# Six x buffers, loads five slots ahead, and a re-ordered beginning in a recurrent block with a looked-up feed-forward part

## The chip, the core and the metric

The kernel runs on one core of one Trainium2 chip. The metric is the device time of one execution in microseconds (us). Before the change the median of three runs is 2197.28 us (2196.02 to 2201.48).

A core has a matrix engine (PE, with its weight loads shown as PEld), VectorE (DVE), ScalarE (ACT), GpSimd (POOL), and SyncE (SP), which here only issues transfers. Each engine works through its own instructions in order. A transfer is issued by one of them (nearly all of them by SP) and is then carried out by the core's 16 DMA engines.

## What is computed

For x of 8 batches with 1024 rows of 512 numbers, cut to what matters:

```python
xn = layernorm(x)
q = xn @ Wq;  gate = softmax(xn @ Wg)
for i in range(3):
    k, v = xn @ Wk[i], xn @ Wv[i]
    w = decay[i] ** max(diff - 1, 0) * (diff > 0)     # diff = s - t, so only later rows count
    blended += gate[..., i:i+1] * (((q @ k.T) * w) @ v)
s = blended @ Wo * out_scale
g = silu(ffn(xn))       # ffn: silu(xn @ lut[gate_idx].T) * (xn @ lut[up_idx].T), then @ lut[down_idx].T
out = x + s * g
```

`lut` has 16 entries. The three feed-forward matrices (1376 x 512, twice, and 512 x 1376) exist only as integer indices into it.

## The kernel before

`phase_1` (L505) computes the attention part of all eight batches and, beside it, builds the feed-forward matrices. `phase_2` (L580) computes the feed-forward part and the result.

**Phase 1 is a hand-written interleaving of Python generators.** A batch has eight tiles of 128 rows (c = 7 down to 0). The loop at L544 runs over batches b = 0 to 8, and inside it the loop at L547 runs over eight slots k. In each slot several generators take a step:

- `newer` is `project(b)` (L278). In slot k it transposes tile c = 7-k (L325, matmuls `pt`, copied to `xnT` by ACT), normalizes tile c-1 (L317), takes the mean and variance of tile c-2 (`statistics`, L299), and loads tile c-3 (`load`, L295). The tiles of x have four buffers (`xp`, L513), so a load can start once the tile four places earlier has been transposed. In a later part of the slot come `features` (L361, matmuls `pq`, from slot 4 on) and `values` (L331, matmuls `pv`). For b = 0, `values` runs one slot late (`lag`). Batch 0 takes statistics and normalizes on DVE, the others on ACT; both use POOL for the reciprocal root (`rstd`).
- `softmax` (L340) turns four tiles' gate logits into weights on DVE and ACT. It then writes them, transposed, to DRAM (`gTd<-g`, L355: 1536 words of 4 bytes) and reads them back broadcast over partitions (`ga<-gTd`, L359).
- `older` is `chunks(b-1)` (L428): the recurrence of the batch before, matmuls `pk`, `psc`, `pu`, `po`. `gated` (L437) multiplies `ga` by q on DVE. The first `psc` of a batch waits for it.
- `ending` is the last part of `project(b-1)` (L415): `features(0, k)`, the sums `ts` for phase 2, and the transfers `xsd<-xnT` and `xsd<-ts` (L424 to L426).
- `following` is `project(b+1)`; it takes its first two steps in slots 6 and 7, and its first step ends in the statistics of its tile 7.
- `setup` is `tables` (L128): the powers of the decay, written to DRAM (`powd<-k_tab`, L152) and read back (`back<-powd`, L158) for `w_tab` and `q_tab`.
- `weights` (L524) builds the matrices: `gate_up_weights` (L205), then `down_weights` (L249). Each tile loads its indices (`idx`, two buffers), looks them up on DVE in 19 steps (`look_up`, L171), makes sums on POOL, and writes to DRAM (`wgud`, `quadd`, `wdd`). `build_some(n)` takes n steps of it.

**Order.** At the end, `keep_order` (L918) ties PE, DVE, ACT and POOL to the order in which Python emitted their instructions. SP is tied only up to L543, before the first slot; the transfers emitted later are put into SP's queue by the scheduler. SP issues its queue strictly in order: a transfer that waits for its data holds up everything behind it.

**Beginning.** L538 to L542 take the first steps: `newer` twice (tiles 7, 6, 5 and 4 are loaded), `more` twice (L91: first `wvg_sb` on ACT's queue, then `wqk_sb` and `wo_sb` on SP's), and `setup` once. From slot 0 on, `weights` takes a step per slot, so the look-up's first instruction (L176) stands on DVE in slot 0.

**Phase 2** begins with the load `xs<-xsd` (L599), whose memory is that of `xnT` and `ts` of phase 1. So it waits for the last `xsd<-ts`.

Of the kernel before, what the change touches and what calls it, by code (L numbers as in the profile page):

```python
# [18 lines left out]
P = 128  # L19
# [19 lines left out]
def recurrent_block(ctx: ExitStack, tc, x, wq, wk, wv, wo, wg, decay_logits, out_scale, lut, gidx, uidx, didx, out):  # L39
# [51 lines left out]
    def more_weights(wvg_sb, wqk_sb):  # L91
        nc.scalar.dma_start(out=wvg_sb[:, :, NI * D :], in_=wg.rearrange("(c p) d -> p c d", p=P))
        for i in range(NI):
            nc.scalar.dma_start(
                out=wvg_sb[:, :, i * D : (i + 1) * D], in_=wv[i].rearrange("(c p) d -> p c d", p=P)
            )
        yield
        nc.sync.dma_start(out=wqk_sb[:, :, :D], in_=wq.rearrange("(c p) d -> p c d", p=P))
        for i in range(NI):
            nc.sync.dma_start(  # L100
                out=wqk_sb[:, :, (i + 1) * D : (i + 2) * D], in_=wk[i].rearrange("(c p) d -> p c d", p=P)
            )
        nc.sync.dma_start(out=wo_sb, in_=wo)


# [22 lines left out]
    def tables():  # L128
# [21 lines left out]
        nc.gpsimd.tensor_tensor(c_tab, dec, e_c, ALU.pow)  # L150
        with nc.allow_non_contiguous_dma(reason="384 words, once"):
            nc.sync.dma_start(out=pow_d[:, P:].rearrange("i s -> s i"), in_=k_tab)  # L152
        for _ in range(3):
            yield
        backs = []
        for step, first in ((1, 0), (0, P)):
# [4 lines left out]
            backs.append(back)  # L161
        for _ in range(2):
            yield
        for tab, back in zip((w_tab, q_tab), backs):
# [39 lines left out]

    def gate_up_weights(build, pool, pair_pool):  # L205

        for o, (s, m) in enumerate(OCH):  # L210
            n = 2 * NV * m
            idx = build.tile([P, NB], I32, name="idx", tag="idx", bufs=2)
            iv = idx[:, :n].rearrange("p (a b) -> p a b", b=m)
            gs, us = (src[:, s : s + m].rearrange("(c p) b -> p c b", p=P) for src in (gidx, uidx))
            nc.sync.dma_start(out=iv[:, 2:6, :], in_=gs)
            nc.sync.dma_start(out=iv[:, 0:2, :], in_=us[:, 0:2, :])
            nc.sync.dma_start(out=iv[:, 6:8, :], in_=us[:, 2:4, :])
            wf = pool.tile([P, 2 * NB], F32, name="wgu", tag="wgu", bufs=2)
            yield from look_up(build, wf[:, :n], idx[:, :n], P, n)
            w = wf[:, : 2 * n].rearrange("p (k two m) -> p k two m", two=2, m=m)  # L220
            a21, a11, a12, a22, s1, s2, s3, s4 = (w[:, k] for k in range(8))
            nc.gpsimd.tensor_tensor(s1, a21, a22, ALU.add)
            nc.gpsimd.tensor_tensor(s2, s1, a11, ALU.subtract)
            yield
            nc.gpsimd.tensor_tensor(s3, a11, a21, ALU.subtract)
            nc.gpsimd.tensor_tensor(s4, a12, s2, ALU.subtract)
            nc.sync.dma_start(out=wgu_d[o], in_=wf[:, 2 * m : 2 * n].rearrange("p (a b) -> p a b", b=m))
            if o < 4 * NQ:
                if o % 2 == 0:
                    upper = w[:, 1:]  # L230
                    continue
                lower = w[:, 1:]
                to = quad_d[o // 4][:, :, o // 2 % 2, :].rearrange("p k (t m) -> p k t m", m=P)
                pair = pair_pool.tile([P, 7, 4, P], F32, name="pair", tag="pair")
                nc.sync.dma_start(out=to[:, :, 0:2, :], in_=upper)
                nc.sync.dma_start(out=to[:, :, 2, :], in_=lower[:, :, 1, :])
                b21, b22, b11, b12 = lower[:, :, 0], lower[:, :, 1], upper[:, :, 0], upper[:, :, 1]
                nc.gpsimd.tensor_tensor(pair[:, :, 0], b21, b22, ALU.add)
                yield
                nc.gpsimd.tensor_tensor(pair[:, :, 1], pair[:, :, 0], b11, ALU.subtract)  # L240
                yield
                nc.gpsimd.tensor_tensor(pair[:, :, 2], b11, b21, ALU.subtract)
                yield
                nc.gpsimd.tensor_tensor(pair[:, :, 3], b12, pair[:, :, 1], ALU.subtract)
                nc.sync.dma_start(out=to[:, :, 3:7, :], in_=pair)
                for _ in range(3):
                    yield

    def down_weights(build, pool):  # L249

        s, m = OCH[-1]
        idx = build.tile([P, NB], I32, name="idx", tag="idx", bufs=2)
        nc.sync.dma_start(out=idx[:m, :V], in_=didx[s : s + m, :])
        wf = pool.tile([P, 2 * NB], F32, name="wgu", tag="wgu", bufs=2)
        yield from look_up(build, wf[:m, :V], idx[:m, :V], m, V)
        nc.sync.dma_start(out=wdt_d, in_=wf[:m, :V])
        for j in range(NK):
            idx = build.tile([P, NB], I32, name="idx", tag="idx", bufs=2)
            for a in range(2):
                nc.sync.dma_start(out=idx[:, ts(a, V)], in_=didx[ts(j + a * NK, P), :])  # L260
            t = pool.tile([P, 2 * NB], F32, name="wgu", tag="wgu", bufs=2)
            yield from look_up(build, t[:, : 2 * V], idx, P, 2 * V)
# [5 lines left out]
            nc.gpsimd.tensor_tensor(t4, b21, t2, ALU.subtract)  # L268
            nc.sync.dma_start(out=wd_d[j], in_=t[:, : 7 * V // 2])

# [7 lines left out]
    def project(b, pools, sides, kept):  # L278
# [61 lines left out]
        def softmax(hf):  # L340
# [12 lines left out]
            nc.vector.tensor_tensor(g, g, sm.to_broadcast([P, n, NI]), ALU.mult)  # L353
            with nc.allow_non_contiguous_dma(reason="1536 words"):
                nc.sync.dma_start(  # L355
                    out=gT_d[b][ts(hf, n * NI), :].rearrange("k p -> p k"), in_=g.rearrange("p c i -> p (c i)")
                )
            gates.append(att.tile([P, n * NI, P], F32, name=f"ga{b}_{hf}", tag="ga"))
            nc.sync.dma_start(out=gates[-1], in_=gT_d[b][ts(hf, n * NI), :].partition_broadcast(P))  # L359

# [11 lines left out]

        load(NC - 1)
        if b > 0:
            load(NC - 2)
            statistics(NC - 1)
        yield
        if b == 0:
            load(NC - 2)
        load(NC - 3)  # L380
        if b == 0:
            load(NC - 4)
            statistics(NC - 1)
        normalize(NC - 1)
# [3 lines left out]
        for k in range(NC):  # L388
            c = NC - 1 - k
            transpose(c)  # L390
            if c > 0:
                normalize(c - 1)
            if c > 1:
                statistics(c - 2)
            if c > 2 and (b, k) != (0, 0):
                load(c - 3)
            if b == 0 and k == 0:
                warm_up(5)
            yield
            if k >= NC // 2:  # L400
                features(1, k - NC // 2)
            half = softmax(1) if k == NC // 2 + lag else iter(())
            next(half, None)
            yield
            next(half, None)
            if k >= lag:
                values(c + lag)
            if lag and k == NC - 1:
                values(0)
            yield  # L410
# [14 lines left out]
        nc.sync.dma_start(out=xs_d[b][:, 4:6, :], in_=b22)  # L425
        nc.sync.dma_start(out=xs_d[b][:, 6:14, :], in_=ts_.rearrange("p a b u -> p (a b) u"))  # L426

# [77 lines left out]
    def phase_1():  # L505
        nonlocal small, p_a, p_c, p_r
        with (
# [4 lines left out]
            tc.tile_pool(name="tp", bufs=1) as tp,  # L512
            tc.tile_pool(name="xp", bufs=4) as xp,  # L513
            tc.tile_pool(name="wts", bufs=1) as wts,
# [8 lines left out]
            pools = (xp, xnp, tp, att)  # L523
            weights = chain(gate_up_weights(build, wgup, pairp), down_weights(build, wgup))  # L524
            wvg_sb = wts.tile([P, NV, NI * D + NI], F32, name="wvg_sb", tag="wvg_sb")
# [15 lines left out]
            next(setup)  # L541
            next(more, None)  # L542
            keep_order(tc, seen, (mybir.EngineType.SP,))  # L543
            for b in range(B + 1):  # L544
                following = project(b + 1, pools, (wvg_sb, wqk_sb), kept) if b + 1 < B else iter(())
                older = chunks(b - 1, (chk, blp), kept) if b else iter(())
                for k in range(NC):  # L547
                    next(older, None)
                    next(newer, None)
                    next(setup, None)  # L550
                    busy = (b > 0 or k >= NC // 2) and b < B
                    build_some(1 + (0 < b < B))
                    if k < NC // 2:
# [8 lines left out]
                    if k >= NC - 2:  # L562
                        next(following, None)
                    next(newer, None)
                    next(older, None)
                for g in (older, ending):
                    for _ in g:
                        pass
                ending, newer = newer, following
            for _ in weights:  # L570
                pass


# [386 lines left out]
```

## Time and profile before

| what | value |
|---|---|
| median of three runs | 2197.28 us |
| the profiled execution: its own time | 2197.51 us |
| its span, first to last instruction | 2195.7 us |
| PE busy | 2171.0 us, 99% |
| DVE, ACT, POOL busy | 51%, 38%, 42% |
| first feed-forward matmul of phase 2 (`fs`) | 627.53 us |
| first matmul that multiplies data (`pt`) | 6.08 us |

All positions below are us from the span's start. The windows view gives the busy time of each engine in a stretch, with its number of instructions, and then the granted PE clock (1.00 is full speed), the busy share of the DMA engines and GB/s. The chain of waits goes back from the last instruction to what released each step. A timeline row is start, length, engine, line, operation, output<-input and shapes; a bracket gives the idle time before it and what ended it.

### The profile page before, as it was taken

How to read it: one execution, taken by the hardware profiler on the slowest of the kernel's cores; microseconds unless marked ns; L12 is line 12 of the kernel's file. 1: busy time of each engine (PE TensorE's matmuls, PEld its weight loads, DVE VectorE, ACT ScalarE, POOL GpSimd, SP SyncE). 2: the span in 40 equal slices, each digit the busy share in tenths (PEclk: the TensorE clock that was granted, in tenths of full speed). 3: DMA queues.
4: the chain of work that ended last, by engine and by line, in shares of the span. 5: the costliest groups of instructions: out<-in, count | busy, mean ns of one | idle time of the engine just before them, and what ended most of it. 6: DMA issues, size and time to landing. Idle time of an engine off the chain costs nothing.

```text
span 2195.7 us, 25271 instructions
## 1 busy us (share of the span) xinstructions
PE 2171.0 (99%) x9234; PEld 1599.3 (73%) x9234; DVE 1111.9 (51%) x1589; ACT 830.0 (38%) x1795; POOL 912.6 (42%) x800
## 2 busy tenths in 40 slices
PE   8989999999999999999999999999999999999998
PEld 5656666666668778678858876885787678578867
DVE  5866868688635534433533443353344335433533
ACT  3556666666434214312421441243144124313410
POOL 2525454334243454424525441543445153434512
PEclk9999999999999999999999999999999999999999
DMA  5766655534284424334432442343244234234501
GB/s 140 203 160 212 162 163 181 181 125 170 83 327 151 149 99 154 114 115 139 161 122 82 153 130 106 132 155 105 105 154 147 106 116 151 89 132 147 164 24 53
DMA packets 137153, 305.29 MB, mean 139 GB/s; under 512 B 50147, under 2 KB 71910, under 8 KB 136006
## 3 DMA queue, kind: packets, MB, share of 16 engines
q1 hardware_dynamic: 127190, 279.03, 39.1%
q0 software_dynamic: 7728, 23.86, 3.0%
q8 instruction: 73, 1.20, 0.2%
q10 hardware_dynamic: 2112, 0.79, 0.1%
q14 instruction: 50, 0.41, 0.1%
HBM read 225.72 MB, written 77.93 MB: 138 GB/s over the span
## 4 chain that ended last, share of the span: by engine, by line
PE 94%; DMA 3%; DVE 1%; POOL 1%; issue 1%; ACT 1%; ACTq 0%; SPq 0%; POOLq 0%; DVEq 0%
PE s L677 27%; PE ds L821 22%; PE fs L631 9%; PE pq L368 8%; PE pv L335 6%; PE sE L677 4%; PE fsE L631 4%; PE po L488 3%; PE ds L832 2%; PE ps L843 2%; PE psc L466 2%; PE pu L474 1%; PE pt L328 1%; DMA x<-in_x 1%; PE pk L457 1%; DMA xs<-xsd 1%
## 5 line engine op out<-in xcount | busy, mean ns | idle before, releaser
L677 PE MATMUL s<-xs,wq 128*128 128x256 f32 x2688 | 602.9, 380 | 0.0
L677 PEld LDWEIGHTS s<-xs,wq 128*128 128x128 f32 x2688 | 508.7, 190 | 78.4 <-DVE sE L704 2.7
L821 PE MATMUL ds<-wd,s 128*128 128x256 f32 x1280 | 286.7, 379 | 0.0
L821 PEld LDWEIGHTS ds<-wd,s 128*128 128x128 f32 x1280 | 243.2, 190 | 33.0
L368 PE MATMUL pq<-xnT,wqk_sb 128*128 128x512 f32 x512 | 230.3, 592 | 0.0
L821 PE MATMUL ds<-wd,h 128*128 128x256 f32 x960 | 222.9, 379 | 0.0
L821 PEld LDWEIGHTS ds<-wd,h 128*128 128x128 f32 x960 | 182.3, 190 | 52.5 <-issue 27.0
L631 PE MATMUL fs<-xs,wr 128*128 128x512 f32 (+1 forms) x480 | 215.4, 592 | 0.3 <-DMA xs<-xsd 0.3
L733 POOL TENSOR_TENSOR u<-u,e 128x512 f32<-128x512 f32 x64 | 79.9, 1270 | 276.0 <-DVE u L729 276.0
L335 PE MATMUL pv<-wvg_sb,xnT 128*128 128x387 f32 x512 | 179.6, 493 | 7.4 <-ACT xnT L329 7.4
L700 DVE TENSOR_TENSOR s<-s,e 128x512 f32<-128x512 f32 x112 | 78.4, 700 | 187.6 <-ACT s L699 187.6
L631 PEld LDWEIGHTS fs<-xs,wr 128*128 128x128 f32 (+1 forms) x480 | 86.8, 181 | 116.1 <-issue 112.4
L368 PEld LDWEIGHTS pq<-xnT,wqk_sb 128*128 128x128 f32 x512 | 92.3, 190 | 91.8 <-issue 91.8
L846 POOL TENSOR_TENSOR gx<-gx 128x512 f32<-128x512 f32 x63 | 80.3, 1275 | 184.6 <-DVE gx L844 141.1
L335 PEld LDWEIGHTS pv<-wvg_sb,xnT 128*128 128x128 f32 x512 | 93.8, 193 | 63.2 <-ACT xnT L329 7.6
L314 POOL TENSOR_SCALAR rstd<-rstd 128x1 f32<-128x1 f32 x56 | 26.9, 481 | 258.8 <-ACT junk L313 258.2
L615 POOL TENSOR_TENSOR xs<-xs 128x1792 f32<-128x1792 f32 (+1 forms) x38 | 127.9, 3382 | 7.6 <-issue 6.6
L704 DVE TENSOR_TENSOR sE<-s,e 128x512 f32<-128x512 f32 x112 | 78.3, 699 | 85.9 <-PE s L677 85.9
L862 ACT ACTIVATE gx<-ds 128x256 f32<-128x256 f32 x32 | 12.3, 384 | 287.1 <-PE ds L832 287.1
L677 PE MATMUL sE<-xs,wq 128*128 128x256 f32 x448 | 115.0, 379 | 0.0
L695 ACT COPY e<-sE 128x512 f32<-128x512 f32 x112 | 65.6, 586 | 123.7 <-PE sE L677 123.7
L737 POOL TENSOR_TENSOR h<-h,e 128x512 f32<-128x512 f32 x64 | 80.0, 1273 | 57.4 <-issue 46.4
(146 smaller groups left out, 3248.6 us busy)
## 6 DMA issues: line engine op xcount, KB each, us to landing
wq<-quadd SPq DMA_DIRECT2D x112, 896.0 KB, 4.5
xs<-xsd SPq DMA_DIRECT2D x8, 3584.0 KB, 12.1
x<-in_x SPq DMA_DIRECT2D x64, 256.0 KB, 5.2
xsd<-ts SPq DMA_DIRECT2D x8, 2048.0 KB, 7.8
gx<-in_x SPq DMA_DIRECT2D x64, 256.0 KB, 2.9
out<-gx POOLq DMA_DIRECT2D x63, 256.0 KB, 2.3
wr<-wgud SPq DMA_DIRECT2D x16, 896.0 KB, 4.6
ga<-gTd SPq DMA_DIRECT2D x16, 768.0 KB, 5.1
```

The costliest lines, as they stand in the source:

```text
L335: nc.tensor.matmul(pv, lhsT=xnT[:, v, ts(c, P)], rhs=wvg_sb[:, v, :], start=(v == 0), stop=(v == NV - 1))
L368: nc.tensor.matmul(pq, lhsT=wqk_sb[:, v, ts(j, D)], rhs=xnT[:, v, ts(hf, U)], start=(v == 0), stop=(v == NV - 1))
L488: nc.tensor.matmul(po, lhsT=lh, rhs=rh, start=(n == 0), stop=(n == len(prods) - 1))
L615: nc.gpsimd.tensor_tensor(o, x1, x2, ALU.subtract)
L631: nc.tensor.matmul(ps, lhsT=w[:, 2 * W_OF[k] + n, :m], rhs=xs[:, X_OF[k], 2 * n : 2 * n + 2, :], start=start and n == 0, stop=stop and n == 1,
L677: nc.tensor.matmul(self.t[n][:, ts(a, H)], lhsT=self.w[:, a, (0, 1, 6, 2, 3, 4, 5)[i - 1], :], rhs=self.xs[:, X_OF[self.k], D_OF[i], :], s ...
L700: nc.vector.tensor_tensor(self.t[1], self.t[1], self.e, ALU.add)
L704: nc.vector.tensor_tensor(self.t[3], self.t[2], self.e, ALU.add)
L733: nc.gpsimd.tensor_tensor(o[:, n], o[:, n], other[:, n], ALU.add)
L737: nc.gpsimd.tensor_tensor(of_h(half, n), of_h(half, n), two(other[:, n]), ALU.mult)
L821: nc.tensor.matmul(ps, lhsT=lhs[k][:, n, :], rhs=wd_sb[n][:, ts(D_OF[k], H)], start=start and n == 0, stop=stop and n == NK - 1, skip_grou ...
L846: (nc.vector if end else nc.gpsimd).tensor_tensor(g, g, xr, ALU.add)
```

## The change

The pool of x goes from four to six buffers, and `load_to(c - 5)` takes the place of `load(c - 3)`; batch 0 loads its tiles 3, 2 and 1 in slot 1 and tile 0 in slot 2. The index loads of a tile are emitted when the tile before it begins. `more` is taken apart: `wqk_sb` is emitted in slot 1, `wo_sb` in slot 3. `weights` takes no step in slot 0. In batch 0 the one-slot lag of `values` ends in slot 4, and with it the first softmax moves from slot 5 to slot 4. Writes to DRAM and the reading back of the gates go through `defer(n, ...)`: they are emitted n ticks later, with three ticks a slot. SP's order is tied up to the end of slot 3 in place of up to the first slot. The compute instructions are the same ones.

```diff
@@ more_weights
         yield
+        yield
         nc.sync.dma_start(out=wqk_sb[:, :, :D], in_=wq.rearrange("(c p) d -> p c d", p=P))
...
+        yield
+        yield
         nc.sync.dma_start(out=wo_sb, in_=wo)
+    later = []
+
+    def defer(parts, issue):
+        later.append([parts, issue])
+
+    def tick():
+        for entry in later:
+            entry[0] -= 1
+        for entry in [e for e in later if e[0] <= 0]:
+            later.remove(entry)
+            entry[1]()
@@ tables
-                nc.sync.dma_start(out=pow_d[:, P:].rearrange("i s -> s i"), in_=k_tab)
-        for _ in range(3):
+        defer(4, write)
+        for _ in range(4):
             yield
...
-        for _ in range(2):
-            yield
+        yield
@@ ffn_weights (was gate_up_weights and down_weights)
             nc.sync.dma_start(out=iv[:, 6:8, :], in_=us[:, 2:4, :])
+            yield
             wf = pool.tile([P, 2 * NB], F32, name="wgu", tag="wgu", bufs=2)
...
-            nc.sync.dma_start(out=wgu_d[o], in_=wf[:, 2 * m : 2 * n].rearrange("p (a b) -> p a b", b=m))
+            defer(3, lambda: nc.sync.dma_start(out=wgu_d[o], in_=wide))
...
+            defer(4, lambda: nc.sync.dma_start(out=to[:, :, 3:7, :], in_=pair))
...
+            defer(3, lambda: nc.sync.dma_start(out=wd_d[j], in_=t[:, : 7 * V // 2]))
+
+        jobs = [gate_up(o) for o in range(NO)] + [down_tail()] + [down(j) for j in range(NK)]
+        next(jobs[0])
+        yield
+        for job, following in zip(jobs, jobs[1:] + [iter(())]):
+            next(following, None)
+            yield from job
@@ project: softmax
+            defer(2, write)
+            defer(6, lambda: nc.sync.dma_start(out=ga, in_=there.partition_broadcast(P)))
@@ project
-        load(NC - 1)
+        ahead = NC - 1
+
+        def load_to(c):
+            nonlocal ahead
+            while ahead >= max(c, 0):
+                load(ahead)
+                ahead -= 1
+
+        if b == 0:
+            load_to(NC - 1)
+            yield
+            load_to(NC - 4)
+        else:
+            load_to(NC - 4)
+        statistics(NC - 1)
         if b > 0:
-            load(NC - 2)
-            statistics(NC - 1)
-        yield
...
+            yield
+            load_to(NC - 5)
         normalize(NC - 1)
...
-            if c > 2 and (b, k) != (0, 0):
-                load(c - 3)
+            if (b, k) != (0, 0):
+                load_to(c - 5)
...
             if k >= NC // 2:
+                if lag and k == NC // 2:
+                    values(c + 1)
+                    lag = 0
                 features(1, k - NC // 2)
-            half = softmax(1) if k == NC // 2 + lag else iter(())
+            half = softmax(1) if k == NC // 2 else iter(())
...
-            if lag and k == NC - 1:
-                values(0)
...
-        nc.sync.dma_start(out=xs_d[b][:, 6:14, :], in_=ts_.rearrange("p a b u -> p (a b) u"))
+        defer(2, lambda: nc.sync.dma_start(out=xs_d[b][:, 6:14, :], in_=ts_.rearrange("p a b u -> p (a b) u")))
@@ phase_1
-            tc.tile_pool(name="xp", bufs=4) as xp,
+            tc.tile_pool(name="xp", bufs=6) as xp,
...
-            next(more, None)
-            keep_order(tc, seen, (mybir.EngineType.SP,))
             for b in range(B + 1):
...
                 for k in range(NC):
+                    tick()
                     next(older, None)
                     next(newer, None)
                     next(setup, None)
                     busy = (b > 0 or k >= NC // 2) and b < B
-                    build_some(1 + (0 < b < B))
+                    build_some((b, k) > (0, 0) and 1 + (0 < b < B))
+                    next(more, None)
+                    tick()
...
+                    tick()
                     next(newer, None)
                     next(older, None)
+                    if (b, k) == (0, 3):
+                        keep_order(tc, seen, (mybir.EngineType.SP,))
...
             for _ in weights:
                 pass
+            while later:
+                tick()
```

More of the change, by code (lines that the diff above doesn't have):

```diff
@@ L1 @@
 from contextlib import ExitStack
-from itertools import chain
 import concourse.bass as bass
@@ L150, in tables, with write @@
         nc.gpsimd.tensor_tensor(c_tab, dec, e_c, ALU.pow)
-        with nc.allow_non_contiguous_dma(reason="384 words, once"):
-            nc.sync.dma_start(out=pow_d[:, P:].rearrange("i s -> s i"), in_=k_tab)
-        for _ in range(3):
+        def write():
+            with nc.allow_non_contiguous_dma(reason="384 words, once"):
+                nc.sync.dma_start(out=pow_d[:, P:].rearrange("i s -> s i"), in_=k_tab)
+        defer(4, write)
+        for _ in range(4):
             yield
@@ L203, in look_up, with ffn_weights, gate_up @@
         yield from tree(dst, 3, 0)
-    def gate_up_weights(build, pool, pair_pool):
-        for o, (s, m) in enumerate(OCH):
+    def ffn_weights(build, pool, pair_pool):
+        upper = []
+        def gate_up(o):
+            s, m = OCH[o]
             n = 2 * NV * m
@@ L226, in gate_up_weights @@
             nc.gpsimd.tensor_tensor(s4, a12, s2, ALU.subtract)
-            nc.sync.dma_start(out=wgu_d[o], in_=wf[:, 2 * m : 2 * n].rearrange("p (a b) -> p a b", b=m))
[L228 to L238, printed above, removed]
-                yield
-                nc.gpsimd.tensor_tensor(pair[:, :, 1], pair[:, :, 0], b11, ALU.subtract)
-                yield
[L242 to L257, printed above, removed]
+            wide = wf[:, 2 * m : 2 * n].rearrange("p (a b) -> p a b", b=m)
+            defer(3, lambda: nc.sync.dma_start(out=wgu_d[o], in_=wide))
@@ new lines, in gate_up @@
+            if o >= 4 * NQ:
+                return
+            if o % 2 == 0:
+                upper.append(w[:, 1:])
+                return
+            up, low = upper.pop(), w[:, 1:]
+            to = quad_d[o // 4][:, :, o // 2 % 2, :].rearrange("p k (t m) -> p k t m", m=P)
+            pair = pair_pool.tile([P, 7, 4, P], F32, name="pair", tag="pair")
+            nc.sync.dma_start(out=to[:, :, 0:2, :], in_=up)
+            defer(3, lambda: nc.sync.dma_start(out=to[:, :, 2, :], in_=low[:, :, 1, :]))
@@ new lines, in gate_up @@
+            b21, b22, b11, b12 = low[:, :, 0], low[:, :, 1], up[:, :, 0], up[:, :, 1]
+            nc.gpsimd.tensor_tensor(pair[:, :, 0], b21, b22, ALU.add)
+            yield
+            nc.gpsimd.tensor_tensor(pair[:, :, 1], pair[:, :, 0], b11, ALU.subtract)
+            yield
+            nc.gpsimd.tensor_tensor(pair[:, :, 2], b11, b21, ALU.subtract)
+            yield
+            nc.gpsimd.tensor_tensor(pair[:, :, 3], b12, pair[:, :, 1], ALU.subtract)
+            defer(4, lambda: nc.sync.dma_start(out=to[:, :, 3:7, :], in_=pair))
@@ new lines, in gate_up, with down_tail, down @@
+            for _ in range(3):
+                yield
+        def down_tail():
+            s, m = OCH[-1]
+            idx = build.tile([P, NB], I32, name="idx", tag="idx", bufs=2)
+            nc.sync.dma_start(out=idx[:m, :V], in_=didx[s : s + m, :])
+            yield
+            wf = pool.tile([P, 2 * NB], F32, name="wgu", tag="wgu", bufs=2)
+            yield from look_up(build, wf[:m, :V], idx[:m, :V], m, V)
+            defer(2, lambda: nc.sync.dma_start(out=wdt_d, in_=wf[:m, :V]))
+        def down(j):
@@ L260, in down_weights @@
                 nc.sync.dma_start(out=idx[:, ts(a, V)], in_=didx[ts(j + a * NK, P), :])
+            yield
             t = pool.tile([P, 2 * NB], F32, name="wgu", tag="wgu", bufs=2)
@@ L268, in down_weights @@
             nc.gpsimd.tensor_tensor(t4, b21, t2, ALU.subtract)
-            nc.sync.dma_start(out=wd_d[j], in_=t[:, : 7 * V // 2])
+            defer(3, lambda: nc.sync.dma_start(out=wd_d[j], in_=t[:, : 7 * V // 2]))
+        jobs = [gate_up(o) for o in range(NO)] + [down_tail()] + [down(j) for j in range(NK)]
+        next(jobs[0])
+        yield
+        for job, following in zip(jobs, jobs[1:] + [iter(())]):
+            next(following, None)
+            yield from job
     def warm_up(n):
@@ L353, in softmax, with write @@
             nc.vector.tensor_tensor(g, g, sm.to_broadcast([P, n, NI]), ALU.mult)
[L354 to L357, printed above, removed]
             gates.append(att.tile([P, n * NI, P], F32, name=f"ga{b}_{hf}", tag="ga"))
-            nc.sync.dma_start(out=gates[-1], in_=gT_d[b][ts(hf, n * NI), :].partition_broadcast(P))
+            there = gT_d[b][ts(hf, n * NI), :]
+            def write():
+                with nc.allow_non_contiguous_dma(reason="1536 words"):
+                    nc.sync.dma_start(out=there.rearrange("k p -> p k"), in_=g.rearrange("p c i -> p (c i)"))
+            ga = gates[-1]
+            defer(2, write)
+            defer(6, lambda: nc.sync.dma_start(out=ga, in_=there.partition_broadcast(P)))
         def features(hf, j):
@@ L371, in features @@
             nc.scalar.copy(qT[hf] if j == 0 else kT[hf][:, j - 1, :], pq)
-        load(NC - 1)
-        if b > 0:
-            load(NC - 2)
-            statistics(NC - 1)
[L377 to L383, printed above, removed]
+        ahead = NC - 1
[6 more added lines that the diff above has]
+            load_to(NC - 1)
+            yield
+            load_to(NC - 4)
+        else:
+            load_to(NC - 4)
+        statistics(NC - 1)
+        if b > 0:
+            yield
+            load_to(NC - 5)
         normalize(NC - 1)
@@ L523, in phase_1 @@
             pools = (xp, xnp, tp, att)
-            weights = chain(gate_up_weights(build, wgup, pairp), down_weights(build, wgup))
+            weights = ffn_weights(build, wgup, pairp)
             wvg_sb = wts.tile([P, NV, NI * D + NI], F32, name="wvg_sb", tag="wvg_sb")
```

## The prediction

> **What bounds the kernel now.** I read the page first, for the engine that sets the time:
>
> ```profile
> PE 2171.0 (99%) x9234; PEld 1599.3 (73%) x9234; DVE 1111.9 (51%) x1589; ACT 830.0 (38%) x1795; POOL 912.6 (42%) x800
> ...
> PEclk9999999999999999999999999999999999999999
> ```
>
> PE is busy for 99% at a full granted clock; nothing else exceeds 51%. The change touches no matmul, so all it can win is PE's idle time, and only in phase 1, whose generators it edits. From 131 us to 600 us the waits view holds a single PE wait, 1.3 us; the stretch 450 to 500 is busy for 50.00 of 50 us. So everything lies before 131 us, or at the handover to phase 2. PE's timeline shows the early gaps (in brackets):
>
> ```profile
> 13.71 0.63 PE L328 MATMUL pt<-ident,x 128*128 128x128 f32 x4 [2.15 <-DVE x L320]
> ...
> 21.87 0.63 PE L328 MATMUL pt<-ident,x 128*128 128x128 f32 x4 [1.88 <-DVE x L320]
> ...
> 58.12 0.94 PE L466 MATMUL psc<-ga,kT 128*128 128x128 f32 x6 [2.84 <-DVE ga L441]
> ```
>
> DVE's own timeline says why x was late:
>
> ```profile
> 12.41 0.69 DVE L176 TENSOR_SCALAR bit<-idx 128x1024 uint8<-128x1024 uint8 x1 [2.90 <-DMA idx<-in_uidx]
> ...
> 18.97 0.69 DVE L305 BATCH_NORM_STATS2 st<-x 128x6 f32<-128x512 f32 x1 [2.85 <-DMA x<-in_x]
> ```
>
> First the look-up stood in front of tile 5's normalization, waiting for indices; then tile 3 itself came late. The chain of waits (start, length, what) gives the rest, and the price of each matmul group:
>
> ```profile
> 41.02 10.66 DMA gTd<-g
> 51.70 5.43 DMA ga<-gTd
> ...
> 68.81 2.61 PE pv L335 x8
> ...
> 73.75 0.44 PE pt L328 x4
> 74.19 3.44 PE pq L368 x8
> ...
> 104.32 13.90 DMA x<-in_x
> ```
>
> The gates' write and reading back end at 57.13 and release the `psc` of 58.12. The load of 104.32 is the large case. SP's timeline around it:
>
> ```profile
> 103.69 0.51 SPq L245 DMA_DIRECT2D quadd<-pair  x1
> 104.32 0.58 SPq L297 DMA_DIRECT2D x<-in_x  x1
> ```
>
> SP had waited 10.1 us for `pair`, with tile 0 of batch 1 behind it, and then the load ran behind 1792 KB of `pair`: 13.90 us against a median of 5.2. ACT stood 11.79 us at that tile's statistics; behind it in ACT's order stood the copy of `xnT` for the next `pv`. The windows (busy us per engine, then granted clock):
>
> ```profile
> 110.00:120.00 10.00, 6.24 (x34) 4.13 (x32) 9.13 (x11) 1.72 (x5) 0.10 (x1) 1.00 1.06 94
> 120.00:130.00 10.00, 6.33 (x21) 4.15 (x22) 2.24 (x2) 6.92 (x19) 7.64 (x10) 0.66 0.65 198
> ```
>
> PE stops for over 7 us, then restarts at a granted clock of 0.66.
>
> **The beginning, step by step.** Tiles 7 and 6 are handled as before: PE's first `pv` ends at 8.79 + 2.61 = 11.40. Without a look-up in slot 0, tile 5's normalization needs only its `rstd` (POOL, 9.34 + 0.60), so it runs at about 10.0 to 10.5 and PE goes on at 11.40 (before: 13.71, so 2.31 us). In the new SP order the zeros for `powd` wait for POOL's memset (7.75 + 0.20), so tiles 3, 2 and 1 are issued at about 8.4, 8.9 and 9.3 (before: 14.17, 14.6 and 25.14), then three index loads until about 10.8, then `wqk_sb` from 11.2 (before 10.48). Tile 3 lands at about 13 (the fastest x load took 4.2 us), the indices at about 15.5. Issue to landing before was 4.4 us for the last of them. The first look-up now stands on DVE in slot 2; behind it stands the normalization of tile 3, done by about 16.3. PE needs that at 17.50 (two rounds of 0.44 + 2.61 after 11.40). If the indices take 3 us longer, up to 2 us come back. So the second gap, 21.87 - (17.22 + 2.61) = 2.04 us, goes, and the third (35.33 against 34.85: 0.48 us, tile 1 issued at 25.14) too. Sum 4.83 us. `wqk_sb` is 0.7 us later in SP's queue, but `pq` comes after `pv` in slot 4 now, at about 20.6; it has some 9 us from issue where the first `wqk` load took 4.5. What is late next: nothing until the gates.
>
> **The gates of batch 0.** All of batch 0's matmuls then run densely: 17.50 + (0.44 + 2.61 + 3.44 + 2.61) for slot 4, + 3 x 6.49 for slots 5 to 7, ends at 46.1 (before: 50.9). `psc` follows `pk` (0.33), `pt` and `pq`: at 50.3. The gates leave DVE at about 26 (before 40.9), because softmax needs `pv` of tile 4, done at 20.6, and ACT's exponent follows `pq`'s copy at 24.5. SP may hold up to three things in front: the reading back of `powd`, whose write took 8.40 us and starts at about 17, and its second transfer (2.63 us on SP), so the write starts at about 29 to 31; plus 10.66 and 5.43 is 45 to 47. DVE needs 0.92 more. Margin about 2.5 us, so the wait of 58.12 - (51.68 + 3.43) = 3.01 us goes. Bounds: from nothing gained (gates read back behind another wait) to 3.01; I take 3.0. The 0.83 us gap before the first `po` (63.00) I leave in.
>
> A rule speaks against this step. The Trainium skill, "DMA: Bandwidth & Descriptors", section "Queues, rings and completion order", says that each DMA engine takes the descriptors of a ring in order and that SP has one row of rings. So x loads that the deeper buffer lets through early stand ahead of the gates' write. By its fabric ceiling of 435 GB/s, four tiles (1 MB) would cost an estimated 2.4 us. The row weighs more: 13.90 - 5.2 = 8.7 us behind 1792 KB, or about 5 us for 1 MB. By the rule the margin holds; by the row the gates come 2.5 us late and most of the 3.0 is lost. The loads may be issued during the wait for `powd`, before the gates exist, so I keep 3.0 and give its loss to the range.
>
> **The stall in batch 1.** Tile 0's buffer was tile 4's, free after its transpose in slot 3 (83.5); with six it is tile 6's, free in slot 1 (64.5): two slots, or 19 us, earlier. SP has openings at 76.4 and 78.6, so the load lands by about 90, and ACT needs it at 106.4. Even a second wait like the one for `pair` fits in. The stall goes whole: 123.67 - (115.41 + 0.67) = 7.59 us, and the slow restart.
>
> For the restart there are again row and rule. Row: the `pv` after the stall took 5.05 us where 2.61 is usual, 2.44 us lost. The Trainium skill, "TensorE: Matmul & The Clock Gate", section "What's actually happening", has half clock until one busy window of about 3.4 us: an estimate of 1.7 us. I take the row: 7.59 + 2.44 = 10.0 us.
>
> **The rest.** Look-up work is the same, two steps of `weights` later: its POOL and DVE instructions fall elsewhere in the slots. The 1.3 us wait at 185.97 (`qb` on POOL behind `pair`) may go, or come at each of the four pairs: -1.3 to +3.9, taken 0. DVE has room (43.2 of 50 us from 60 to 110, PE not waiting). Deferred writes hold `wgu` up to one slot longer, and its next writer comes some 20 steps later, over three slots; `idx` had two buffers already. At the handover, `xsd<-ts` (606.93, 7.2 us) and `xs<-xsd` (13.29) release `fs` at 627.53, where PE idled only 0.27 us: this chain is as long as PE's own. It starts from PE's progress, so it moves along, but a look-up before `ts` (1.25 us) or a write put ahead of it on SP counts in full. Bounds: -0.3 to +7 (the wait for the last `wdd` write, 621.01 - 614.20, placed before `xs`); taken 0.
>
> **Sum**: 4.83 + 3.0 + 10.0 = 17.8 us off the profiled execution's 2197.51 (its span of 2195.7 and 1.8 around it), so 2179.7. The median of the runs, 2197.28, differs by 0.2. I predict 2180.
>
> **Rivals.**
> - Beginning gained, a late x stays (10%): SP still gets stuck, another tile takes tile 0's place. For it: SP waits 160 us in all for gate writes before their reading back. Against: 19 us of lead exceed each single wait (longest 13.6). 2197.5 - 7.8 = 2189.7.
> - Stall gone, beginning not (11%): indices and gates late, DVE waiting in slot 2 as it did in slot 0. For it: DMA share 1.02 from 10 to 20 us. 2197.5 - 10.0 = 2187.5.
> - Slower (15%): the scheduler puts the reading back of the gates, which holds SP for 10.7 us, in front of an x load that is due: tile 7 of the next batch, emitted in slot 6 right before its statistics. ACT absorbed 11.8 - 7.4 = 4.4 us in the stall above, so each case costs 10.7 + 5.2 - 4.4 = 11.5, and 2.4 for the restart: 13.9 us. Two of seven batches turn the sign: 2179.7 + 27.8 = 2207.5. Against: before, SP issued x at 104.32 ahead of gates emitted earlier (105.42), so loads go out when their buffer is free, now sooner. It decides when a load is issued less than 1 us before its statistics are reached.
> - No change (8%): the deferred `xsd<-ts` falls behind the last `bld<-bl` (623.54): 17 us and a restart of 2.4 eat the gain: 2199. Against: before, it was emitted after that write too and still went first.
>
> **Chances.** This kernel's measurement can tell 0.3%, 6.6 us, from no change. My forecast has 56%; with the first two rivals faster is 77%, same 8%, slower 15%. The range: best case 17.8 + 1.3 + 0.8 + 0.6 = 20.5, so 2177, with 1 us for runs; above, the two partial gains and some POOL waits, 2193. The likeliest case alone is 2176 to 2184.
>
> **What would show it.** PE's `pt` of tile 5 at about 11.4, of tile 3 at about 17.5; `psc` at about 50; no ACT wait for x in batch 1 and a granted clock of 1.00 from 100 to 130; `fs` at about 610. Wrong if ACT or DVE waits for x in later batches, if SP's wait for gate writes has an x load behind it that is due, or if `xs<-xsd` starts after the last `po`.

## The result, and the profile after

| | before | after |
|---|---|---|
| median | 2198.13 us (4 runs, 2196.02 to 2201.48) | 2179.88 us (4 runs, 2178.10 to 2179.93) |
| profiled execution | 2197.51 us | 2179.92 us |
| first feed-forward matmul of phase 2 | 627.53 us | 610.05 us |

The ratio is 0.9914 (95% interval 0.9896 to 0.9931), a gain of 0.9%. Of the 17.6 us between the two profiled executions, 17.5 are already there when phase 2 starts. So the gain lies in phase 1.

The page after:

```profile
PE 2167.8 (100%) x9234; PEld 1599.0 (73%) x9234; DVE 1117.3 (51%) x1589; ACT 830.1 (38%) x1795; POOL 918.3 (42%) x800
```

PE's timeline after, at the places of the early gaps (tiles 5 and 3 of batch 0, then the first `psc` and the first `po`):

```profile
11.37 0.60 PE L363 MATMUL pt<-ident,x 128*128 128x128 f32 x4
...
17.46 0.60 PE L363 MATMUL pt<-ident,x 128*128 128x128 f32 x4
...
50.19 0.83 PE L513 MATMUL psc<-ga,kT 128*128 128x128 f32 x6
...
55.83 0.94 PE L535 MATMUL po<-pr,v 128*128 128x128 f32 x6 [1.53 <-DVE pr L515]
```

The brackets of the first three are gone. At the `po` a gap has grown from 0.67 to 1.53 us. The windows over the former stall:

```profile
110.00:120.00 10.00, 10.00 (x48) 6.59 (x47) 7.46 (x9) 4.45 (x12) 2.52 (x2) 1.00 0.55 153
120.00:130.00 10.00, 10.00 (x49) 6.71 (x48) 8.74 (x17) 6.23 (x17) 6.84 (x8) 1.00 0.58 214
```

PE is busy for 10.00 of 10 us in both, and the clock stays at 1.00. ACT no longer waits for x in batch 1. SP's timeline after has the load of tile 0 of batch 1 long ahead of the `pair` write, and no longer 0.6 us behind it:

```profile
60.13 0.91 SPq L332 DMA_DIRECT2D x<-in_x  x1
...
96.95 0.53 SPq L271 DMA_DIRECT2D quadd<-pair  x1
```

DVE's timeline and the chain of waits show where the beginning was tight:

```profile
16.05 0.69 DVE L194 TENSOR_SCALAR bit<-idx 128x1024 uint8<-128x1024 uint8 x1 [2.28 <-DMA idx<-in_uidx]
...
49.39 0.56 DVE L488 TENSOR_TENSOR ga<-ga,qT 128x384 f32<-128x384 f32 x1 [7.78 <-DMA ga<-gTd]
```

```profile
17.64 10.51 DMA powd<-k_tab
...
30.30 14.42 DMA gTd<-g
44.73 4.64 DMA ga<-gTd
```

The look-up still waits for its indices, but now with no tile behind it that PE is waiting for yet. The gates land at 49.37 and DVE is done with them at 49.95, only 0.24 us before PE can start `psc`.

### The profile page after: what moved, and what is told of

Read it like the earlier page. It is cut to its first block, busy times and chain, and to the rows that moved or that the text cites. A ratio compares the mean times of both kernels' runs of the same rounds, so it can differ in the third digit from the quotient of the medians.

```text
span 2178.1 us, 25266 instructions
## 1 busy us (share of the span) xinstructions
PE 2167.8 (100%) x9234; PEld 1599.0 (73%) x9234; DVE 1117.3 (51%) x1589; ACT 830.1 (38%) x1795; POOL 918.3 (42%) x800
## 4 chain that ended last, share of the span: by engine, by line
PE 96%; DMA 1%; POOL 1%; issue 1%; DVE 0%; ACT 0%; SPq 0%; POOLq 0%
PE s L730 27%; PE ds L874 22%; PE fs L684 9%; PE pq L407 9%; PE pv L370 7%; PE sE L730 4%; PE fsE L684 4%; PE po L535 4%; PE ds L885 2%; PE ps L896 2%; PE psc L513 2%; PE pu L521 2%; PE pt L363 1%; PE pk L504 1%; DMA gTd<-g 1%
## 5 line engine op out<-in xcount | busy, mean ns | idle before, releaser
L907 DVE TENSOR_TENSOR pw<-ds,pw 128x256 f32<-128x256 f32 x32 | 13.6, 425 | 177.0 <-PE ds L874 177.0
```

## The experiments

The forecast put the gain into three terms: the look-up and the loads at the beginning, the gates, and the stall in batch 1. It gave the last to the two extra buffers (theory A). The rival theory B: what counts is where a load stands in SP's queue, and several edits of this change move it. Times are medians, ratios are to the kernel before on the same chip.

| run | median, us | ratio, 95% interval |
|---|---|---|
| six_alone | 2181.75 | 0.9923 (0.9908 to 0.9938) |
| later_build | 2188.46 | 0.9954 (0.9939 to 0.9969) |
| four_in_after | 2178.54 | 0.9908 (0.9894 to 0.9923) |
| lookup_slot0 | 2182.93 | 0.9928 (0.9912 to 0.9945) |
| four_slot0 | 2180.77 | 0.9912 (0.9896 to 0.9929) |
| softmax_slot5 | 2180.16 | 0.9916 (0.9899 to 0.9932) |
| no_defer | 2191.20 | 0.9970 (0.9958 to 0.9981) |
| powd_now | 2190.98 | 0.9968 (0.9956 to 0.9979) |
| others_now | 2178.88 | 0.9914 (0.9898 to 0.9931) |
| less_build | 2178.56 | 0.9911 (0.9897 to 0.9926) |
| sp_tied | 2304.59 | 1.0481 (1.0465 to 1.0497) |
| tied_not_xsd | 2201.87 | 1.0019 (1.0009 to 1.0028) |

### Buffers, or the place in the queue?

**six_alone**, on the kernel before (`load_to` as in the change):

```diff
-            tc.tile_pool(name="xp", bufs=4) as xp,
+            tc.tile_pool(name="xp", bufs=6) as xp,
...
-            if c > 2 and (b, k) != (0, 0):
-                load(c - 3)
+            if (b, k) != (0, 0):
+                load_to(c - 5)
```

> The kernel before with six x buffers and loads five slots ahead, nothing else. Theory A (the buffers end the batch-1 stall): tile 0's buffer is free two slots earlier, the 10.0 us go, and tile 3 of batch 0 comes early too (about 2.5 us): about 2185 us, no ACT wait for x in batch 1. Theory B (the place in SP's queue decides, whatever moves it): also about 2185. Rival (another transfer takes tile 0's place behind the pair write): 2195 or more.

2181.75 us. The stall is gone, and more of the beginning goes than expected: the first `psc` starts at 52.94 in place of 58.12, 5.2 us earlier and not 2.5. The 2.5 are tiles 3 and 1, which are no longer late. The rest is the wait for the gates, which the expectation left out. SP's and DVE's timelines of the kernel before show why the gates were late there:

```profile
24.66 0.38 SPq L158 DMA_DIRECT2D back<-powd  x1
25.14 0.43 SPq L297 DMA_DIRECT2D x<-in_x  x1
```

```profile
30.09 0.69 DVE L305 BATCH_NORM_STATS2 st<-x 128x6 f32<-128x512 f32 x1 [5.70 <-DMA x<-in_x]
```

The load of tile 1 stood behind the reading back of `powd`, which waited for its write. DVE waited 5.70 us for that tile, and the first softmax stood behind it on DVE. In six_alone tile 1 is issued by 16.2, ahead of that write; the gates leave DVE at 32.6 in place of 41.0, with softmax still in slot 5, and PE doesn't wait for them.

Phase 2 starts 15.3 us earlier (612.2), and the profiled execution gains 15.05 us (2197.51 - 2182.46). So this edit alone has most of the change's 17.6 us. By the medians the rest of the change adds 1.9 us, and the intervals don't part the two. Tile 5's gap, 2.34 us here, is what six_alone leaves in. Both theories expected the end of the stall, so this run doesn't part them.

**later_build**, on the kernel before, still with four buffers:

```diff
-                    build_some(1 + (0 < b < B))
+                    build_some((b, k) > (0, 1) and 1 + (0 < b < B))
```

> The kernel before, four buffers, but no look-up step in slots 0 and 1, so that all building falls two steps later. Theory A (buffers): tile 0 of batch 1 still comes late, about 2197 us. Theory B (place in SP's queue): the pair write is emitted later than that load, the load goes out ahead of it, the stall of 10.0 us is gone: about 2187 us.

2188.46 us: theory B. SP's timeline of this run, where tile 0's load of batch 1 is the first row:

```profile
85.91 0.34 SPq L297 DMA_DIRECT2D x<-in_x  x1
...
106.34 0.53 SPq L245 DMA_DIRECT2D quadd<-pair  x1
```

With the same four buffers the load now goes out 20 us ahead of the `pair` write, because that write is emitted two building steps later. PE's large wait for `xnT` (7.4 us before) is 0.3. The profiled execution gained 7.6 us, not 10 (the medians differ by 10.3): the first `po` came 2.2 us later than before (65.16 against 63.00), after a 4.1 us gap at tile 3, whose load came no earlier than before. From the first `po` to phase 2 it gained 9.6 us.

**four_in_after**, on the changed kernel:

```diff
-            tc.tile_pool(name="xp", bufs=6) as xp,
+            tc.tile_pool(name="xp", bufs=4) as xp,
...
-                load_to(c - 5)
+                load_to(c - 3)
```

(`load_to(NC - 4)` and `load_to(NC - 5)` at a later batch's start become `NC - 2` and `NC - 3`.)

> The changed kernel with four x buffers and loads three slots ahead, all else kept. Theory A (buffers): the stall in batch 1 is back, about 2190 us. Theory B (place in SP's queue): the load of tile 0 stands ahead of the pair write all the same, about 2180 us, and ACT waits for x at most a little.

2178.54 us: theory B again. SP's timeline, tile 0 of batch 1 first:

```profile
74.74 0.34 SPq L332 DMA_DIRECT2D x<-in_x  x1
...
95.19 0.53 SPq L271 DMA_DIRECT2D quadd<-pair  x1
```

The load stands ahead of the `pair` write without the two buffers. Phase 2 starts even a little earlier than in the changed kernel (608.3 against 610.0), though the intervals of the times overlap. The gates' write took 11.5 us from issue to the reading back (29.80 to 41.32) in place of 14.4, and the gap before the first `po` is gone. That the fewer x loads shortened the write is not shown: with six buffers it took from 9.2 (lookup_slot0) to 14.4 us.

**lookup_slot0**, on the changed kernel:

```diff
-                    build_some((b, k) > (0, 0) and 1 + (0 < b < B))
+                    build_some(2 if (b, k) == (0, 0) else 1 + (0 < b < B))
```

> The changed kernel with two building steps back in slot 0 (index loads and the first look-up). Theory (the look-up in front of tile 5's normalization is what held PE): indices land at about 14.5 us, tile 5's transpose goes from 11.4 to about 15.5, and the first psc by as much: about 2184 us. Rival (the gates set the time of the first psc, so slack swallows it): 2180 us, psc still at about 50.

2182.93 us, 3.1 more than the changed kernel. DVE waits 3.5 us for indices in front of tile 5. PE's timeline:

```profile
14.35 0.76 PE L363 MATMUL pt<-ident,x 128*128 128x128 f32 x4 [2.64 <-DVE x L355]
14.90 4.37 PE L370 MATMUL pv<-wvg_sb,xnT 128*128 128x387 f32 x8
```

Tile 5 goes 3.0 us later than in the changed kernel, and a slow restart adds 1.7: these `pv` take 4.37 us where 2.77 is usual, and the granted clock from 14.3 to 19.1 was 0.64. So the first `psc` is at 54.87, 4.7 us later. But the gates have then long landed and the 1.5 us gap at `po` is gone: 58.82 against 55.83.

**four_slot0** joins the edits of four_in_after and lookup_slot0.

> The changed kernel with four x buffers and two building steps back in slot 0: the two edits of four_in_after and lookup_slot0 together. Theory B (place in SP's queue; here the load of tile 0 of batch 1 still stands ahead of the pair write): 2183 us, as with six buffers, no stall in batch 1. Rival (with the building early, as in the kernel before, four buffers give the stall again): about 2192 us.

2180.77 us and no stall: the load of tile 0 goes out at 78.72, the `pair` write at 97.30. In the changed kernel no run with four buffers has lost anything.

### The gates and the first softmax

**softmax_slot5**, on the changed kernel:

```diff
-                if lag and k == NC // 2:
-                    values(c + 1)
-                    lag = 0
...
-            half = softmax(1) if k == NC // 2 else iter(())
+            half = softmax(1) if k == NC // 2 + lag else iter(())
...
+            if lag and k == NC - 1:
+                values(0)
```

> The changed kernel with the one-slot lag of values kept to the end of batch 0, so that the first softmax is in slot 5 again. Theory (the gates' write and reading back decide when the first psc starts): the gates leave DVE some 6 us later, their write starts at about 34 in place of 30, the first psc at 52 to 54 in place of 50.2: about 2183 us. Rival (the powd transfers hold SP anyway, so softmax has slack): 2180 us.

2180.16 us: the rival is right. The gates leave DVE 4 us later (29.45 against 25.45), but their write is issued at 30.24, as in the changed kernel (30.30). In both, SP waits for the `powd` write before its reading back, until 26.98 here and 28.17 there, and then issues other transfers without a pause. Moving softmax a slot earlier brought nothing here.

**less_build** takes the four building steps that stand ahead of `pr` out of slot 0 of batch 1's loop (two behind it stay):

```diff
-                    build_some((b, k) > (0, 0) and 1 + (0 < b < B))
+                    build_some((b, k) > (0, 0) and (b, k) != (1, 0) and 1 + (0 < b < B))
...
-                    build_some(busy * (1 + (b > 0)))
+                    build_some(busy * (1 + (b > 0) - 2 * ((b, k) == (1, 0)) + 1 * ((b, k) in ((1, 1), (1, 2), (1, 3), (1, 4)))))
```

> The changed kernel with no building steps in slot 0 of batch 1's loop; its four steps are made up one each in slots 1 to 4. Theory (the gap before the first po is DVE's look-ups in front of pr): the 1.5 us gap goes or shrinks to latency (0.7), the first po at about 55 in place of 55.8: about 2179 us, no clear difference in time. Rival (gates' landing sets it): same gap.

The first `po` is at 54.68 in place of 55.83 without a gap, and phase 2 starts at 608.9. 2178.56 us: by the intervals not told apart from the changed kernel. The gates also came 0.75 us earlier in this run, but the gap was 1.53: the rest is the steps.

### What deferring is for

**no_defer**, on the changed kernel:

```diff
     def defer(parts, issue):
-        later.append([parts, issue])
+        issue()
```

> The changed kernel with every deferred transfer emitted at once. Theory (deferring is not what wins): only the beginning moves, because the powd write then stands ahead of the index loads in the tied part of SP's queue and they come some 3 us later: PE loses 1 to 2 us at tile 3, about 2181.5 us. Rival (deferring keeps writes out of the x loads' way): ACT waits for x again and 2185 us or more.

2191.20 us. The place was as expected, the size not: PE lost 10.4 us at tile 3. SP's, DVE's and PE's timelines of this run:

```profile
12.97 0.38 SPq L169 DMA_DIRECT2D powd<-k_tab  x1
13.39 0.48 SPq L238 DMA_DIRECT2D idx<-in_gidx  x1
```

```profile
26.75 0.69 DVE L194 TENSOR_SCALAR bit<-idx 128x1024 uint8<-128x1024 uint8 x1 [12.99 <-DMA idx<-in_uidx]
```

```profile
28.04 1.09 PE L363 MATMUL pt<-ident,x 128*128 128x128 f32 x4 [10.43 <-DVE x L355]
```

The index loads were issued by 14.9, only 4 us later than in the changed kernel. But behind the `powd` write they landed at about 26.7, some 12 us after the last issue in place of 5. That write carries 1.5 KB in words of 4 bytes and took 9.1 us, so it landed at 22.1, and the index loads 4.5 us after it.

**powd_now** and **others_now** split that run. The first emits only the `powd` write at once, the second everything but it.

```diff
-        defer(4, write)
+        write()
```

```diff
-    later = []
+    later, done = [], []
...
-        later.append([parts, issue])
+        later.append([parts, issue]) if parts == 4 and not later and not done else issue()
+        done.append(1)
```

> The changed kernel with the powd write alone emitted at once, in slot 1 ahead of the index loads; all other transfers stay deferred. Theory (this one place made the loss seen with nothing deferred: DVE waits 13 us for indices that run behind the powd write): about 2191 us, tile 3's transpose at about 28. Rival (the other deferred writes carry part of it): clearly below 2191.

> The changed kernel with every deferred transfer emitted at once except the powd write, which stays deferred. Theory (deferring pays for the powd write only): 2180 us, tile 3's transpose at about 17.5. Rival: above 2183.

2190.98 and 2178.88 us. All of the loss of no_defer is that one write's place (tile 3's transpose at 28.48, against 17.77 with the others at once). Deferring the other writes brings nothing that these runs can tell.

### How much the scheduler's freedom is worth

**sp_tied**, on the changed kernel:

```diff
-                    if (b, k) == (0, 3):
-                        keep_order(tc, seen, (mybir.EngineType.SP,))
...
     phase_1()
+    keep_order(tc, seen, (mybir.EngineType.SP,))
     phase_2()
```

> The changed kernel with SP's whole queue of phase 1 tied to the order of emission, in place of slots 0 to 3 only. Theory (the scheduler's hoisting of the last xsd writes is needed, the mechanism of the no-change rival): the last xsd writes stand behind the last bl write, the load of xs starts some 17 us later and PE restarts slowly: about 2200 us, and x loads cost nothing more. Rival (order of emission is as good): 2180 us. Second rival (x loads of the next batch come late in every batch, as in the slower rival): 2210 us or more.

2304.59 us, far worse than each theory had it. The waits view of this run, phase 1 (engine, line, waited for: us in all, times, longest):

```profile
DVE ts L464 <- DMA xsd<-ts: 102.0, 7, 15.8
...
PE po L535 <- DVE pr L515: 43.6, 7, 9.7
...
PE pv L370 <- ACT xnT L364: 22.8, 7, 3.7
```

`ts` has one buffer. In the order of emission a batch's `xsd<-ts` stands behind the batch's last `bld<-bl`, so the next batch's first sum for `ts` waits for it on DVE, seven times, and `pr` and PE wait behind. At the handover PE waits 26.0 us more, for the first `wr`. With the 43.6 and the 22.8 that makes 92 us of waiting. Slow restarts come on top: the granted clock from 0 to 600 was 0.95.

**tied_not_xsd** ties the same queue but leaves the `xsd` writes to the scheduler: they go through a helper that adds their names to `seen`.

```diff
-        nc.sync.dma_start(out=xs_d[b][:, 0:4, :], in_=xnT[:, :, :U])
...
+        def untied(**kw):
+            had = len(nc.cur_bb.bb.instructions)
+            nc.sync.dma_start(**kw)
+            seen.update(i.name for i in list(nc.cur_bb.bb.instructions)[had:])
+
+        untied(out=xs_d[b][:, 0:4, :], in_=xnT[:, :, :U])
+        untied(out=xs_d[b][:, 4:6, :], in_=b22)
+        defer(2, lambda: untied(out=xs_d[b][:, 6:14, :], in_=ts_.rearrange("p a b u -> p (a b) u")))
```

> The changed kernel with SP's queue of phase 1 tied to the order of emission, as in sp_tied, but with the xsd writes left to the scheduler. Theory (the late xsd writes hold ts and xnT of the next batch on DVE and ACT, and the load of xs at the end; that is nearly all of the 124 us): 2180 to 2190 us. Rival (x loads and gates that come late in every batch are as large): 2230 or more.

2201.87 us, so the `xsd` writes are 102.7 of the 124.7 us that sp_tied lost against the changed kernel. The number expected was missed by 12 us: at the handover the first `wr` was still issued behind the last `wdd` write and PE waited 17.6 us for it. Nothing comparable is left in the batches: ACT waited 16.9 us for x, six times, and PE 0.9 us behind it.

## Why the prediction was right, and where it was not

The time was forecast at 2180 and is 2179.88. By its steps:

- **The beginning**, 4.83 us: measured 4.93 (the first `pk` of batch 1 starts at 45.99, before 50.92). Tile 5 goes at 11.37 (forecast 11.40), tile 3 at 17.46 (17.50). lookup_slot0 shows the mechanism: with the look-up back in slot 0, tile 5 waits for it again.
- **The gates**, 3.0 us: measured 3.00 (58.12 - 50.19 = 7.93, less 4.93). That it came whole was luck. The write of the gates took 14.42 us and not 10.66. The reserve for such a delay was put at 2.5 us, and 0.24 was left. The row about x loads around a transfer had priced this risk at 5 us, and the write was 3.8 longer; but whether x loads made it longer is open. Nor was softmax's earlier slot a cause (softmax_slot5). What freed the gates was tile 1's load, no longer behind the `powd` write: six_alone has the gain too, and in later_build, where tile 1 still goes out at 25.92, the gates leave DVE at 42.0 and PE waits 2.5 us for them.
- **The gap before the first `po`**, left in: it grew by 0.86. DVE, held until 49.39 by the gates, had a building step, `ts` and two look-ups in front of `pr`. It takes both, late gates and steps: it is gone without the steps (less_build), and also with them where DVE gets the gates at 45.46 (four_in_after) or 46.48 (others_now).
- **The stall**, 10.0 us: the size fits, with one slip. The 2.44 for the restart compare a whole `pv` of 5.05 us with the distance of two starts, 2.61; whole against whole (2.77) it is 2.28, so the stall cost 9.87. From the first `po` (7.17 us earlier than before) to phase 2 (17.48) another 10.3 us are gained; 0.3 of them is the wait in front of `fs`. The step that fails is "Tile 0's buffer was tile 4's, free after its transpose in slot 3; with six it is tile 6's": the buffers are enough for it (six_alone), but within this change not needed (four_in_after, four_slot0), and building two steps later was enough as well (later_build). What held the load was the write in front of it in SP's queue.
- **The restart**: neither the row nor the rule is a constant. After the 10.4 us gap of no_defer, `pt` and `pv` took 5.47 us from 28.04 to 33.51 where 3.05 is usual: 2.42 lost. Shorter gaps lost about the rule's 1.7 (last section). The forecast needed only the loss in the kernel before, and took it from its trace.
- **The no-change rival** had a real mechanism, and it is the one that the scheduler's freedom keeps away. Its price was taken for the handover alone; tied in every batch it is over 100 us.

## What to carry to other kernels

When a load comes late, look first at what stands in front of it on the issuing queue. A deeper buffer moves the load ahead, but so may an edit that moves the write. Keep small writes of scattered words out of the way of loads that are due: here 1.5 KB held the index loads back by some 7 us. Before an order of transfers is tied down by hand, ask for every single-buffered tile when its next writer comes.

## What the runs showed of the hardware that was not expected

- A write of 384 words of 4 bytes took 8.40 us (before), 9.1 (no_defer) and 10.51 (after). Index loads issued behind it on the same queue landed late with it: in some 12 us, where 5 is usual (no_defer).
- The gates' write of 1536 such words took 10.66 us before and 14.42 in the changed kernel. In other runs with six buffers it took 14.2 (softmax_slot5), 13.0 (less_build), 11.8 (others_now), 9.65 (six_alone) and 9.2 (lookup_slot0), in the two with four in the changed kernel 11.5. What sets it was not found.
- What PE lost at its restart did not grow steadily with the gap. It was 2.28 us after 7.4 us (before) and 2.42 after 10.4 (no_defer), with granted clocks of 0.56 and 0.55. After 17.6 us (tied_not_xsd) the first eight `fs` took 5.23 us where 3.43 is usual, 1.80, at 0.66. After 2.6 us (lookup_slot0) it was 1.7, after 4.1 and 2.5 us (later_build) 1.7 and 1.8, at 0.64 to 0.70. After 2.8 us in front of the `psc` of 58.12 (before) it was 0.1, and the clock stayed at 1.00.
